# A filter loop whose transfers are cut into smaller ones and tied to places in the chunk

## The chip, the cores and the metric

The kernel runs on one core of a Trainium2 chip. The metric is the time on the device in microseconds, from one launch to its end. Engines are named as in the profile: PE (TensorE, with PEld for its weight loads), DVE (VectorE), ACT (ScalarE), POOL (GpSimd), SP (SyncE, which here only issues transfers).

## What is computed

The program takes `x` of 8 x 32 x 32 x 128 floats through two layers. Layer 0 is attention over 1024 tokens of each of 8 images. Layer 1 adds a state-space model run in both directions, and then a spectral filter. Only this last part is touched by the change:

```python
def _compute_spectral(u, sigma, phi, Mpp, Mpm):
    U_plus, U_minus = _stu_conv(phi, u, PADDED_SL)
    s = sigma ** SIGMA_POW
    out = jnp.einsum('btkd,k,kde->bte', U_plus, s, Mpp)
    out = out + jnp.einsum('btkd,k,kde->bte', U_minus, s, Mpm)
    return out
...
t = _to_tokens(x)
...
t = t + _L1_ffn_ref(_ln_t(t), L1_ffn_sigma, L1_ffn_phi, L1_ffn_M_u, L1_ffn_M_phi_plus, L1_ffn_M_phi_minus, L1_ffn_log_weights, L1_ffn_gumbel)
x = _from_tokens(t, x)
```

Here `_stu_conv` convolves each channel of the tokens with 16 filters, through Fourier transforms. The sum over filters and input channels may be done at each frequency: for every frequency a 128 x 128 matrix over the channels is applied to the spectra of the tokens, and the result is transformed back.

## The kernel before

The kernel is one straight program of about 47,600 instructions. Its last part, from line 1588 on, is in two stages.

**The filter loop.** The 128 frequencies (`NF`) go in 16 chunks of 8 (`FC`). For a chunk `c` there are two jobs. *Matrices*: `matrices` (line 1600) multiplies the filters' taps with the filter matrices, which lie in `mst`, into PSUM tiles `pg`; four copies per call, alternately by ACT (line 1613) and DVE (line 1611), bring them to SBUF as `gs`. *Apply*: `apply` (line 1634) multiplies the matrices with the spectra `u` into `py`, and `gather` (lines 1649 to 1655) forms sums and differences: one copy by ACT (`half`), then additions by DVE. A pair of gathers makes one tile `sums` of 128 rows, which is written to `yd` in device memory.

The loop runs one chunk ahead with the matrices: in round `c` it makes the matrices of chunk `c + 1` and applies those of chunk `c`. Each round has four steps `n`: two calls of `matrices`, then two of `apply` and one `gather`. Steps 0 and 1 make the first half of the chunk's frequencies, steps 2 and 3 the second. The order on PE, DVE, ACT and POOL is that in which the program is written (`manual_schedule` with these four in `IN_ORDER`); the order on SP is left to a scheduler.

**The loop's transfers, all issued by SP.** Each chunk needs its spectra: two loads of 256 KB (line 1620), each in rows of 256 bytes, after which POOL makes a negated and a plain copy (lines 1623 and 1624, once per chunk over the whole tile). Each chunk stores two tiles of sums of 256 KB (line 1657). When both stores of a chunk have landed, two early reads of 64 KB (line 1665, `fetch`) bring the part of `yd` that the last stage needs first into `early_yt`: 8 partitions per chunk. In the last round, which makes no matrices, the residuals are loaded from `xa`: 2 MB into `res1`, which takes the place of `mst`, and 1 MB into `room`, which takes the place of a `gs` (line 1668).

**The last stage.** After the loop come six reads of 1 MB of `yd` into `room` (line 1709) with one load of 1 MB of residuals among them, the inverse transform on PE (line 1725), the addition of the residuals by DVE (line 1732) and five stores of the output, issued by ACT (line 1735).

A tile's tag has so many buffers: `gs` and `u` two, `sums` three. A transfer that fills a buffer waits for its last readers.

Of the kernel before, what the change touches and what calls it, by code (L numbers as in the profile page):

```python
# [10 lines left out]
ALU = mybir.AluOpType  # L11
# [4 lines left out]
B = 8  # L16
# [14 lines left out]
NB = 2  # L31
NF = 128
FC = 8
PI_1024 = 0.0030679615757712823
IN_ORDER = {
    mybir.EngineType.PE,
    mybir.EngineType.DVE,
    mybir.EngineType.Activation,
    mybir.EngineType.Pool,
}  # L40
ALL_IN_ORDER = IN_ORDER | {mybir.EngineType.SP}
# [4 lines left out]
def fast_kernel(ctx: ExitStack, tc: tile.TileContext, a: dict, out: bass.AP, bad: bass.AP):  # L46
    nc = tc.nc
# [15 lines left out]
    def ctile(shape, name):  # L63
        pool = passing
        if name in LASTING:
            pool = const
        elif name in ("fwd", "m_u"):
            pool = resid
        elif name in ("wqkv", "bout", "group", "row_le", "row_ge"):
            pool = starting  # L70
        return pool.tile(shape, F32, tag=name, name=name)
# [8 lines left out]
    ud = dram.tile([NF // FC, P, B, NB, 2, 4, FC], F32, name="ud")  # L80
    yd = dram.tile([NF, NB, B, 2, 4, C], F32, name="yd")
# [23 lines left out]
    for d, m in enumerate((row_le, row_ge)):  # L105
        t = ctile([P, L], f"upto{d}")
        for c in range(2):
            rows = slice(c * L, (c + 1) * L)
# [504 lines left out]
    with ExitStack() as s:  # L613
# [172 lines left out]
        sums = {}  # L786
# [85 lines left out]
        for n in range(len(units) + 2):  # L872
            if n < len(units):
                prs[n] = scores(*units[n])
            if 2 <= n and units[n - 2][2] % 2:
                b, half, j = units[n - 2]
# [3 lines left out]
            if 1 <= n < len(units) + 1:  # L880
                b, half, j = units[n - 1]
# [42 lines left out]
    with ExitStack() as s:  # L924
# [12 lines left out]
        for d in range(2):  # L937
            nc.gpsimd.memset(up[d], 0.0)
            for c in range(2):
                rows = slice(c * L, (c + 1) * L)  # L940
# [57 lines left out]
        def behind(instruction, other, reason):  # L998
            tc.add_manual_dep(
                instruction.ins,  # L1000
                other.ins.name,
                mybir.DependencyInfo(mybir.DependencyClass.Sync, mybir.DependencyReason.DATA),
                reason=reason,
            )
# [360 lines left out]
        for at, u in enumerate(units[:-1]):  # L1365
# [41 lines left out]
            b = (u.b + 2) % B  # L1407
# [34 lines left out]
        u = units[-1]  # L1442
# [71 lines left out]
    with ExitStack() as s:  # L1514
        mp = s.enter_context(tc.tile_pool(name="c_m", bufs=1, side="right"))
        mst = mp.tile([P, 32, C], F32, tag="mst", name="mst")
        early_yt = mp.tile([P, 2, 4, 4, C], F32, name="early_yt")
# [67 lines left out]
        with ExitStack() as s2:  # L1585
# [4 lines left out]
            turn = 0  # L1590

            def matrices(c, n, gs):

                nonlocal turn
                pts = [ps_g.tile([P, 4, P], F32, tag="g", name=f"pg{c}_{n}_{g}") for g in range(4)]
                cols = slice(c * FC, (c + 1) * FC)
                for e in range(4):
                    for g in range(4):
                        rows = slice(g * 32, (g + 1) * 32)
                        nc.tensor.matmul(  # L1600
                            pts[g][:, e, :],
                            lhsT=mst[rows, n * 4 + e, :],
                            rhs=taps[rows, cols].rearrange("p f q m i -> p (f q m i)"),
                            start=True,
                            stop=True,
                        )
                for g, pt in enumerate(pts):
                    to = gs[:, :, n * 16 + g * 4 : n * 16 + g * 4 + 4]
                    frm = pt.rearrange("p e n -> p n e")
                    if turn % 2:  # L1610
                        nc.vector.tensor_copy(to, frm)  # L1611
                    else:
                        nc.scalar.copy(to, frm)  # L1613
                    turn += 1

            def loaded_spectra(c):

                u = p2.tile([P, 2, NB, B, 2, 4 * FC], F32, tag="u", name=f"u{c}")
                for k in range(NB):
                    nc.sync.dma_start(  # L1620
                        u[:, 0, k].rearrange("p b i f -> p b (i f)"), ud[c][:, :, k].rearrange("p b i q f -> p b (i q f)")
                    )
                nc.gpsimd.tensor_scalar(u[:, 1, :, :, 0, :], u[:, 0, :, :, 1, :], -1.0, None, ALU.mult)  # L1623
                nc.gpsimd.tensor_copy(u[:, 1, :, :, 1, :], u[:, 0, :, :, 0, :])
                return u

            def apply(c, n, q, gs, u, py):

                mats = gs.rearrange("p (f q m i) e -> p f q m i e", f=FC, q=4, m=NB)
                for m in range(NB):  # L1630
                    for i in range(2):
                        for t in range(4):
                            f = n * 4 + t
                            nc.tensor.matmul(  # L1634
                                py[t * 32 : t * 32 + 32 - 16 * m, q // 2, :],
                                lhsT=u[:, i, m:, :, :, q * FC + f].rearrange("p k b i -> p (k b i)"),
                                rhs=mats[:, f, q, m, i, :],
                                start=(m == 0 and i == 0),
                                stop=(m == NB - 1 and i == 1),
                            )  # L1640

            def gather(c, n, turn, py):

                if turn == 0:
                    gathered["sums"] = p3.tile([P, 4, C], F32, tag="sums", name=f"sums{c}_{n}")
                    gathered["both"] = p2.tile([P, 2, C], F32, tag="both", name=f"both{c}_{n}")
                sums, both = gathered["sums"], gathered["both"]
                half = p2.tile([P, C], F32, tag="half", name=f"half{c}_{n}_{turn}")
                nc.scalar.copy(half, py[:, 1, :])
                nc.vector.tensor_tensor(both[:, turn, :], py[:, 0, :], half, ALU.add)  # L1650
                nc.vector.tensor_tensor(sums[:, 2 + turn, :], py[:, 0, :], half, ALU.subtract)
                if turn == 0:
                    return
                nc.vector.tensor_tensor(sums[:, 0, :], both[:, 0, :], both[:, 1, :], ALU.add)
                nc.vector.tensor_tensor(sums[:, 1, :], both[:, 0, :], both[:, 1, :], ALU.subtract)
                at = c * FC + n * 4
                nc.sync.dma_start(
                    yd[at : at + 4].rearrange("f k b i q e -> (f k b i) (q e)"), sums.rearrange("p q e -> p (q e)")
                )

            def fetch(c):

                rows = slice(c * FC, (c + 1) * FC)
                for i in range(2):
                    nc.sync.dma_start(early_yt[rows, i], yd[rows, 0, 0:4, i])

            def load_residuals(k, b, n):
                nc.sync.dma_start(  # L1668
                    res[k][:, b : b + n].rearrange("p b r c -> p b (r c)"),
                    xa[b : b + n, :, k].rearrange("b p r c -> p b (r c)"),  # L1670
                )

            chunks = NF // FC
            gs, us, gathered = {}, {}, {}
            s2.enter_context(tc.manual_schedule(engines=IN_ORDER))
            for c in range(-1, chunks):
                if c + 1 < chunks:
                    gs[c + 1] = p2.tile([P, P, C], F32, tag="gs", name=f"gs{c + 1}")
                    us[c + 1] = loaded_spectra(c + 1)
                else:  # L1680

                    room = p2.tile([P, P, C], F32, tag="gs", name="room")
                    res = [room[:, :32, :], mp.tile([P, 32, C], F32, tag="mst", name="res1")]
                    res = [t.rearrange("p (b r) c -> p b r c", b=B) for t in res]
                    load_residuals(1, 0, B)
                    load_residuals(0, 0, 4)

                for n in range(4):
                    if c + 1 < chunks:
                        matrices(c + 1, 2 * n, gs[c + 1])  # L1690
                        matrices(c + 1, 2 * n + 1, gs[c + 1])
                    if c >= 0:
                        half, turn = divmod(n, 2)
                        py = ps_g.tile([P, 2, C], F32, tag="g", name=f"py{c}_{n}")
                        apply(c, half, turn, gs[c], us[c], py)
                        apply(c, half, turn + 2, gs[c], us[c], py)
                        gather(c, half, turn, py)
                if c > 0:
                    fetch(c - 1)
            fetch(chunks - 1)  # L1700


            pieces = [(k, h) for k in range(NB) for h in range(2)]
# [8 lines left out]
            for yt, (k, h) in zip(yts, pieces):  # L1712
# [6 lines left out]
                for b in range(0, 4, size):  # L1719
                    bs = slice(b, b + size)  # L1720
                    to = res[blk][:, h * 4 + b : h * 4 + b + size]
# [825 lines left out]
```

## Time and profile before

| | us |
|---|---|
| median of 3 runs | 1401.35 |
| the three runs | 1397.77, 1401.35, 1403.96 |
| the profiled execution, own time | 1397.79 |
| its span, first to last instruction | 1396.1 |
| before the filter loop | 0 to 1071.6 |
| filter loop, first matrices to the end of the last product | 1071.6 to about 1352 |
| last stage | about 1352 to 1396.1 |

The span is the time from the first to the last instruction of the profiled execution; 1.7 us lie around it. A line of groups names line, engine and operation, then what is written and read. In a line of the time line the columns are start, duration, engine, line, operation, how many instructions are merged, and in brackets the idle time before it with what ended it; "issue" there means that the profile shows nothing that the engine waited for. DMA queue q1 carries the transfers that SP issues, q8 instructions. These are the sizes of the loop's transfers:

```profile
u<-ud SPq DMA_DIRECT2D x32, 256.0 KB
yd<-sums SPq DMA_DIRECT2D x32, 256.0 KB
...
early_yt<-yd SPq DMA_DIRECT2D x32, 64.0 KB
res<-xa SPq DMA_DIRECT2D x1, 2048.0 KB
room<-xa SPq DMA_DIRECT2D x2, 1024.0 KB
```

### The profile page before, as it was taken

How to read it: one execution, taken by the hardware profiler on the slowest of the kernel's cores; microseconds unless marked ns; L12 is line 12 of the kernel's file. 1: busy time of each engine (PE TensorE's matmuls, PEld its weight loads, DVE VectorE, ACT ScalarE, POOL GpSimd, SP SyncE). 2: the span in 40 equal slices, each digit the busy share in tenths (PEclk: the TensorE clock that was granted, in tenths of full speed). 3: DMA queues.
4: the chain of work that ended last, by engine and by line, in shares of the span. 5: the costliest groups of instructions: out<-in, count | busy, mean ns of one | idle time of the engine just before them, and what ended most of it. 6: DMA issues, size and time to landing. Idle time of an engine off the chain costs nothing. (4 is left out here: it accounts for less than half of the span.)

```text
span 1396.1 us, 47569 instructions
## 1 busy us (share of the span) xinstructions
PE 1322.0 (95%) x20926; PEld 840.1 (60%) x20926; DVE 1094.0 (78%) x2140; ACT 926.1 (66%) x1432; POOL 534.1 (38%) x510
## 2 busy tenths in 40 slices
PE   7999999999999899999999999998798999999977
PEld 3333333333333666666666666666698988888964
DVE  6789888788778698989889888997554777777745
ACT  5767667766766788888878888875553655555520
POOL 3312976886910443434343343443673111111100
PEclk9999999999999999999999999999999999999989
DMA  7200111111101434444444443431578122222358
GB/s 173 56 2 2 39 39 39 54 39 39 31 1 40 99 79 95 112 96 109 94 108 92 93 94 91 115 83 47 166 220 219 45 71 72 72 71 72 79 179 303
DMA packets 139391, 123.24 MB, mean 88 GB/s; under 512 B 44808, under 2 KB 118152, under 8 KB 135080
## 3 DMA queue, kind: packets, MB, share of 16 engines
q1 hardware_dynamic: 137048, 115.93, 32.4%
q8 instruction: 166, 2.72, 0.8%
q10 hardware_dynamic: 2128, 4.19, 0.8%
q14 instruction: 49, 0.40, 0.1%
HBM read 78.15 MB, written 34.08 MB: 80 GB/s over the span
## 5 line engine op out<-in xcount | busy, mean ns | idle before, releaser
L803 ACT ACTIVATE pr<-pt 128x1024 f32<-128x1024 f32 x256 | 248.0, 1021 | 103.1 <-PE pt L798 102.1
L1613 ACT COPY gs<-pg 128x512 f32<-128x512 f32 x256 | 133.2, 601 | 69.9 <-PE pg L1600 54.8
L1611 DVE COPY gs<-pg 128x512 f32<-128x512 f32 x256 | 159.1, 684 | 20.6 <-PE pg L1600 16.7
L828 DVE TENSOR_TENSOR two<-pr,pr 128x1024 f32<-128x1024 f32 x128 | 164.3, 1324 | 13.4 <-ACT pr L803 13.4
L798 PE MATMUL pt<-q,k 32*128 32x512 f32 x1024 | 160.3, 640 | 6.1 <-ACT pr L803 4.2
L1600 PE MATMUL pg<-taps,mst 32*128 32x128 f32 x4096 | 149.2, 281 | 7.8 <-issue 4.6
L1600 PEld LDWEIGHTS pg<-taps,mst 32*128 32x128 f32 x4096 | 134.7, 188 | 22.4 <-issue 17.3
L819 PE MATMUL po<-pr,v 128*32 128x512 f32 x1024 | 139.9, 604 | 0.0
L1634 PE MATMUL py<-gs,u 128*32 128x128 f32 (+1 forms) x4096 | 129.9, 280 | 2.3 <-issue 2.2
L1024 POOL TENSOR_TENSOR ec<-ec,ct 128x2048 f32<-128x2048 f32 x16 | 83.6, 5228 | 112.4 <-ACT ct L1104 49.8
L1066 DVE SCALAR_TENSOR_TENSOR xs<-xp,cw,xs 128x1024 f32<-128x1024 f32 x96 | 122.4, 1282 | 2.2 <-issue 0.2
L1634 PEld LDWEIGHTS py<-gs,u 128*32 128x32 f32 (+1 forms) x4096 | 113.6, 141 | 10.1 <-issue 2.8
L1088 PE MATMUL pb<-bxt,wbc 128*128 128x512 f32 x256 | 114.0, 597 | 3.6 <-ACT zs L1079 3.6
L1623 POOL TENSOR_SCALAR u<-u 128x512 f32<-128x512 f32 x16 | 24.0, 1500 | 233.0 <-DMA u<-ud 121.1
L798 PEld LDWEIGHTS pt<-q,k 32*128 32x128 f32 x1024 | 49.0, 183 | 88.8 <-ACT pr L803 27.5
L1187 DVE SCALAR_TENSOR_TENSOR state<-state,dec,pst 128x64 f32<-128x64 f32 x448 | 87.3, 275 | 1.1
L1296 POOL TENSOR_TENSOR rms<-rms_v,mhalf 128x8 f32<-128x8 f32 x16 | 27.2, 1698 | 156.6 <-DVE rms_v L1294 156.6
L1088 PEld LDWEIGHTS pb<-bxt,wbc 128*128 128x128 f32 x256 | 47.1, 189 | 60.4 <-issue 55.0
L819 PEld LDWEIGHTS po<-pr,v 128*32 128x32 f32 x1024 | 27.7, 109 | 88.1 <-issue 84.8
L1010 POOL TENSOR_TENSOR lm<-cs,lm 128x2048 f32<-128x2048 f32 x16 | 57.9, 3621 | 58.1 <-DVE xs L1066 34.7
L839 PE MATMUL pd<-two,ones 128*32 128x512 f32 x512 | 74.0, 614 | 2.4 <-DVE two L828 2.2
L1266 PEld LDWEIGHTS spo<-wo,y 128*128 128x128 f32 x512 | 62.1, 191 | 15.3 <-issue 10.2
(305 smaller groups left out, 2768.9 us busy)
## 6 DMA issues: line engine op xcount, KB each, us to landing
lm<-cd SPq DMA_DIRECT2D x32, 512.0 KB
ec<-cd SPq DMA_DIRECT2D x32, 512.0 KB
ud<-sp SPq DMA_DIRECT2D x8, 1024.0 KB
u<-ud SPq DMA_DIRECT2D x32, 256.0 KB
yd<-sums SPq DMA_DIRECT2D x32, 256.0 KB
moved<-state SPq DMA_DIRECT2D x48, 128.0 KB
room<-yd SPq DMA_DIRECT2D x6, 1024.0 KB
X<-in_x SPq DMA_DIRECT2D x8, 512.0 KB
```

What stands on the lines that cost most here:

```text
L798: nc.tensor.matmul(pt[:, i, :], lhsT=k[rows, j * P : (j + 1) * P], rhs=q[rows, cols], start=True, stop=True)
L803: nc.scalar.activation(pr[:, 2 * g : 2 * g + 2, :].rearrange("p i t -> p (i t)"), pt.rearrange("p i t -> p (i t)"), AF.Exp, scale=SCALE,)
L819: nc.tensor.matmul(po[rows, :], lhsT=vs[b][:, j, rows], rhs=pr[:, h, :], start=(j == 0), stop=(j == NT - 1))
L828: nc.vector.tensor_tensor(two, sums["pr"][:, 2 * g : 2 * g + 2, :], pr[:, 2 * g : 2 * g + 2, :], ALU.add)
L1024: t = nc.gpsimd.tensor_tensor(u.ec, u.ec, u.ct.unsqueeze(1).to_broadcast([P, NH, NT, L]), ALU.mult)
L1066: u.convolved = nc.vector.scalar_tensor_tensor(acc, xp[:, at : at + T], cw[u.d][:, n, i : i + 1], acc, ALU.mult, ALU.add)
L1088: nc.tensor.matmul(u.pb[:, i * 512 : (i + 1) * 512], lhsT=wbc[u.d][:, k, :], rhs=xt[:, at : at + 512], start=(k == 0), stop=(k == KC - 1),)
L1187: nc.vector.scalar_tensor_tensor(u.state[:, k, h, :], u.state[:, k - 1, h, :], u.dec[:, c, h, j : j + 1], u.pst[c][:, j, h, :], ALU.mult, ...
L1600: nc.tensor.matmul(pts[g][:, e, :], lhsT=mst[rows, n * 4 + e, :], rhs=taps[rows, cols].rearrange("p f q m i -> p (f q m i)"), start=True, ...
L1611: nc.vector.tensor_copy(to, frm)
L1613: nc.scalar.copy(to, frm)
L1634: nc.tensor.matmul(py[t * 32 : t * 32 + 32 - 16 * m, q // 2, :], lhsT=u[:, i, m:, :, :, q * FC + f].rearrange("p k b i -> p (k b i)"), rhs ...
```

## The change

Each transfer of the loop is made smaller or single, and is given a place. A round has eight slots, two for each step `n`: slot `2n` follows the matrices' copies, slot `2n + 1` the gather. `passing_by` issues what belongs to the slot. `behind` adds a wait of the transfer for the copy named: in an even slot the last copy of the matrices, in an odd one ACT's copy of `half`.

- The spectra of the next chunk come in four loads of 128 KB (one of two blocks, one half of the batch), in slots 1, 2, 4 and 5. After each, POOL makes the negated and the plain copy of that quarter. Before, a chunk's spectra could be loaded as soon as the buffer was free.
- The sums are stored in two halves of 64 rows (128 KB): the first half at once in slots 3 and 7 (without an added wait), the second half in slot 6, and in slot 0 of the next round.
- The early reads of the chunk before go one by one, in slots 2 and 4.
- The residuals go in six loads of 512 KB, one in each of the last round's first six slots. That round makes no matrices, so its even slots have no copy to wait for.
- SP's instructions now keep the order in which the program is written (`ALL_IN_ORDER`).

```diff
+            def behind(instruction, other):
+                tc.add_manual_dep(
+                    instruction.ins,
+                    other.ins.name,
+                    mybir.DependencyInfo(mybir.DependencyClass.Sync, mybir.DependencyReason.DATA),
+                    reason="spaced transfers",
+                )
...
-                for k in range(NB):
-                    nc.sync.dma_start(
-                        u[:, 0, k].rearrange("p b i f -> p b (i f)"), ud[c][:, :, k].rearrange("p b i q f -> p b (i q f)")
-                    )
-                nc.gpsimd.tensor_scalar(u[:, 1, :, :, 0, :], u[:, 0, :, :, 1, :], -1.0, None, ALU.mult)
-                nc.gpsimd.tensor_copy(u[:, 1, :, :, 1, :], u[:, 0, :, :, 0, :])
...
+            def load_part(u, c, part, other=None):
+            
+                k, h = divmod(part, 2)
+                bs = slice(4 * h, 4 * h + 4)
+                t = nc.sync.dma_start(
+                    u[:, 0, k, bs].rearrange("p b i f -> p b (i f)"), ud[c][:, bs, k].rearrange("p b i q f -> p b (i q f)")
+                )
+                if other:
+                    behind(t, other)
+                nc.gpsimd.tensor_scalar(u[:, 1, k, bs, 0, :], u[:, 0, k, bs, 1, :], -1.0, None, ALU.mult)
+                nc.gpsimd.tensor_copy(u[:, 1, k, bs, 1, :], u[:, 0, k, bs, 0, :])
...
-                at = c * FC + n * 4
-                nc.sync.dma_start(
-                    yd[at : at + 4].rearrange("f k b i q e -> (f k b i) (q e)"), sums.rearrange("p q e -> p (q e)")
-                )
...
+            def store(c, n, h, sums, other=None):
+
+                at = c * FC + n * 4 + 2 * h
+                t = nc.sync.dma_start(
+                    yd[at : at + 2].rearrange("f k b i q e -> (f k b i) (q e)"),
+                    sums[64 * h : 64 * h + 64].rearrange("p q e -> p (q e)"),
+                )
+                if other:
+                    behind(t, other)
...
-            s2.enter_context(tc.manual_schedule(engines=IN_ORDER))
+            s2.enter_context(tc.manual_schedule(engines=ALL_IN_ORDER))
+            late_sums, waiting = {}, []
+
+            def passing_by(c, n, place, made):
+
+                slot = 2 * n + place
+                if slot in (3, 7):
+                    half = n // 2
+                    store(c, half, 0, gathered["sums"])
+                    late_sums[c, half] = (gathered["sums"],)
+                if slot == 6:
+                    store(c, 0, 1, *late_sums.pop((c, 0)), made)
+                if slot == 0 and c > 0:
+                    store(c - 1, 1, 1, *late_sums.pop((c - 1, 1)), made)
+                if c + 1 < chunks and slot in (1, 2, 4, 5):
+                    load_part(us[c + 1], c + 1, (1, 2, 4, 5).index(slot), made)
+                if c > 0 and slot in (2, 4):
+                    fetch(c - 1, (2, 4).index(slot), made)
+                if c + 1 == chunks:
+                    for _ in range(min(1, len(waiting))):
+                        waiting.pop(0)(made)
...
-                    load_residuals(1, 0, B)
-                    load_residuals(0, 0, 4)
+                    for k, b in [(1, 0), (1, 2), (1, 4), (1, 6), (0, 0), (0, 2)]:
+                        waiting.append(lambda made, k=k, b=b: load_residuals(k, b, 2, made))
 
                 for n in range(4):
+                    made = None
                     if c + 1 < chunks:
                         matrices(c + 1, 2 * n, gs[c + 1])
-                        matrices(c + 1, 2 * n + 1, gs[c + 1])
+                        made = matrices(c + 1, 2 * n + 1, gs[c + 1])
                     if c >= 0:
+                        passing_by(c, n, 0, made)
                         half, turn = divmod(n, 2)
                         py = ps_g.tile([P, 2, C], F32, tag="g", name=f"py{c}_{n}")
                         apply(c, half, turn, gs[c], us[c], py)
                         apply(c, half, turn + 2, gs[c], us[c], py)
-                        gather(c, half, turn, py)
-                if c > 0:
-                    fetch(c - 1)
-            fetch(chunks - 1)
+                        made = gather(c, half, turn, py)
+                        passing_by(c, n, 1, made)
+            store(chunks - 1, 1, 1, *late_sums.pop((chunks - 1, 1)))
+            for i in range(2):
+                fetch(chunks - 1, i)
```

## The prediction

> **What bounds the kernel now.** I read the page first (shares and the chain), then the core's spans by stretch, then the waits inside the filter loop, then the time line of single chunks, and last the DMA view of half-microsecond slices of them.
>
> ```profile
> span 1396.1 us, 47569 instructions
> ...
> PE 1322.0 (95%) x20926; PEld 840.1 (60%) x20926; DVE 1094.0 (78%) x2140; ACT 926.1 (66%) x1432; POOL 534.1 (38%) x510
> ...
> PE pg L1600 10%; PE py L1634 9%; PE pf L565 1%; DMA room<-yd 1%; PE pu L595 1%; ACT ln_x L483 1%; PE cpt L554 1%; DVE sd L576 0%; PE pz L1725 0%; SPq L1709 0%; ACT me L1534 0%; DMA xa<-X 0%; DVE b_st L467 0%; SPq L1668 0%; POOL sp L583 0%
> ```
>
> TensorE is the bound, and the two matmul lines of the filter loop (1600, 1634) lead the chain. The change touches only this loop, 1071.6 to 1353 us, and what follows. Cut into chunks (columns: PE, PEld, DVE, ACT, POOL busy, clock, DMA share, GB/s) it shows:
>
> ```profile
> 1094.60:1111.10 16.50, 16.50 (x518) 15.27 (x517) 12.43 (x29) 9.35 (x21) 2.06 (x2) 1.00 0.29 76
> ...
> 1145.30:1162.90 17.60, 17.01 (x522) 15.37 (x518) 12.58 (x29) 9.65 (x21) 2.05 (x2) 1.00 0.27 71
> ...
> 1213.90:1231.60 17.70, 16.87 (x521) 15.31 (x520) 12.56 (x29) 9.36 (x21) 2.07 (x2) 1.00 0.27 70
> ...
> 1300.40:1316.80 16.40, 16.40 (x520) 15.15 (x519) 12.51 (x29) 9.28 (x21) 2.06 (x2) 1.00 0.29 76
> ...
> sum 238.60, PE 233.90 PEld 213.69 DVE 175.61 ACT 131.33 POOL 28.88; mean PE 16.71 PEld 15.26 DVE 12.54 ACT 9.38 POOL 2.06
> ```
>
> A chunk that nothing disturbs takes 16.4 us and fills PE; nine of fourteen take 16.9 to 17.7. 14 x 16.4 = 229.6, so 238.6 - 229.6 = 9.0 us are lost, 4.7 of them as visible PE idle time (238.6 - 233.9). The waits name no engine for it, and one chunk shows it:
>
> ```profile
> PEld pg L1600 <- issue: 17.3, 66, 1.0
> ```
>
> ```profile
> 1138.72 1.16 PE L1600 MATMUL pg<-taps,mst 32*128 32x128 f32 x29
> 1140.67 1.38 PE L1600 MATMUL pg<-taps,mst 32*128 32x128 f32 x35 [0.79 <-issue]
> ```
>
> ```profile
> 1134.77 0.52 SPq L1620 DMA_DIRECT2D u<-ud  x1
> 1136.00 0.34 SPq L1657 DMA_DIRECT2D yd<-sums  x1
> 1136.39 0.52 SPq L1620 DMA_DIRECT2D u<-ud  x1
> 1140.81 0.63 SPq L1665 DMA_DIRECT2D early_yt<-yd  x2
> ```
>
> The gap is in mid-group, its place moves from 35 to 55 matmuls before the group's end over the loop, and it comes about 2 to 5 us after two u loads and a store (768 KB) were issued within 1.6 us. In the DMA view of 1138.0 to 1138.5 the instruction queue appears:
>
> ```profile
> q1 hardware_dynamic: 368, 0.11, 95.0%
> q8 instruction: 1, 0.02, 11.9%
> ```
>
> One such packet comes at 1128.4, 1132.6, then at 1138.2 where about 1136.7 was due: 1.5 us late, behind the burst. PE goes on 2.47 us after the late packet's start. The same holds at 1224.1 (PE again at 1226.69) and 1215.4 (1217.80). So a group of 128 matmuls ends a block of instructions every 4.11 us, a block is usable about 2.5 us after its packet starts, and there are 1139.88 - (1136.7 + 2.5) = about 0.7 us of slack. A burst that holds the packet back longer shows as a stall.
>
> The loop's end, from the chain:
>
> ```profile
> 1343.64 2.24 issue
> 1345.88 5.33 PE py L1634 x106
> ...
> 1352.86 2.24 DMA yd<-sums
> ...
> 1358.19 3.13 SPq L1668
> ...
> 1361.37 2.59 SPq L1709
> ...
> 1364.00 19.07 DMA room<-yd
> ```
>
> Residual loads of 2 MB (issued at 1338.23) and 1 MB (1341.90) saturate the DMA engines until about 1349.5; PE stalls for a block (2.24 us) and restarts on a low clock (0.81, then 0.62). The last sums land at 1352.86 + 2.24 = 1355.1; from there 6 MB of sums and 1 MB of residuals set the end.
>
> **What the Trainium skill says.** "Runtime: NRT & Kernel Launch", Instruction fetch mechanics: instructions come in blocks of 256 (16 KiB) by the sequencer's own DMA queue, the crossing "mostly hidden". The trace agrees on the block (0.02 MB packets) and shows where it isn't hidden. "DMA: Bandwidth & Descriptors", Queues, rings and completion order: each DMA engine serves its rings in turn, packet by packet. The trace has the fetch wait 1.5 us all the same, so I reckon with what is queued ahead. "TensorE: Matmul & The Clock Gate", Part 1: after idling TensorE gets half its clock for some 3.4 us of work; the clock of 0.62 after the 2.24 us stall fits.
>
> **The change part by part.** The instruction order of PE, DVE and ACT is unchanged; SP becomes a written order, POOL gets four pairs of operations per chunk where it had one.
>
> *Loads of spectra.* 2 x 256 KB become 4 x 128 KB, behind slots 1, 2, 4, 5 of the chunk (a slot: after the matrices' last copy, or after the copy of half the sums). Same bytes and 256-byte rows, so no data time is added. SP issues 4 x about 0.3 instead of 2 x 0.52 us and has over 10 us free in a chunk. The first load took from 1136.0 to 1137.2 for 256 KB, so a half is about 0.6 us of the engines. For the block fetch this means: instead of 1.5 us of delay, at most about 0.6, which is just under the slack of 0.7.
>
> *Sums by halves, early reads singly.* 128 KB and 64 KB each, at slots 3, 6, 7, next 0, and 2, 4. A 256 KB store alone delayed one packet (1215.4) into a 0.26 us stall; its half should not. The early reads wait for stores that were issued about 4.6 us before, where a landing takes 2.24 us: no stop for SP.
>
> *What is queued behind these waits.* SP is in order, so a late copy holds up everything behind it, the next chunk's spectra above all. The last quarter is issued 0.4 us after the third matmul group, its data takes about 1.0 to start and 0.6 to move, 0.9 passes until POOL starts (as 1294 to 1296.47 shows), and POOL needs between a quarter of and all of 1500 + 618 ns, 0.5 to 2.1 us; I take 0.95. It is ready 3.9 us after that group and needed 4.11 + 2.17 = 6.3 us after it. Cover 2.4 us; if it is gone, 1 us per us and chunk, 15 times. POOL's idle time (14 of 16.4 us) hides its four pairs at either bound.
>
> *What remains of the stalls.* Two of the four blocks in a chunk meet a half load. Bounds: none left (gain 9.0), or all as now (gain 0). I take 0.07 us for each of 28, 2.0 us, so 7.0 us are gained.
>
> *The start.* The second chunk's spectra are no longer loaded up front (1075) but during chunk 0, when DMA is nearly free: nothing either way.
>
> *The end.* The residual loads come later: SP places the first behind the last store of chunk 14, about 1342.3 instead of 1338.2, in 512 KB pieces. From 1342.5 the engines have to move 0.26 MB of sums, 3.15 of residuals, 0.13 of early reads, 0.26 of sums: 3.8 MB at the 385 to 390 GB/s of these stretches, 9.7 us, and 0.5 for a bubble while SP waits for a landing before the early read; with the last 0.26 MB they end at 1353.4 and land at 1354.4. PE no longer stalls at 1343.64 (its block is asked for at about 1339.7, before any load), so its sums are done by about 1349.1 instead of 1352.8; they then stand behind loads. Hence 0.7 us gained, not 3.7. Bounds -1.5 (the early reads, which fill only 8 partitions, hold the queue) to +1.5. What follows (reads in the same order, 1355.1 to the end) only shifts.
>
> *Sum.* Own time of the profiled execution 1397.79 - 7.0 - 0.7 = 1390.1. It is 3.56 us under the median of 1401.35; if the difference is more of these stalls, it goes too (1390.1), if not, it stays (1393.7). I take the middle, 1391.9.
>
> **The rivals.** A: the stalls stay or move to other blocks, since a fetch now always has some transfer beside it; only the end gains: 1401.35 - 0.7 = 1400.6. For it: half loads start where the fetch packets stand (1.3 to 2.2 us into a group), and the slack is no larger than a half load. Against it: chunks whose packets came ahead of the burst ran at exactly 16.4 us with the same bytes.
>
> B, slower: the half load together with the early read of the slot before it delays the fetch by 1.0 us instead of 0.6, at two blocks of every chunk, also in the five that are now free of stalls. Idle time costs 9.0/4.7 = 1.9 times itself, so 28 x (1.0 - 0.7) x 1.9 = 16 us are lost where 9.0 are now: 1401.35 + 7.0 - 0.7 = 1407.7. It decides from a delay of 0.7 + 9.7/(28 x 1.9) = 0.88 us. For it: the early read goes to 8 partitions and its data straggles for 1.5 us (1141.5 to 1143). Against it: 192 KB in all, spread over two slots.
>
> C: the last quarter lands over 2.4 us late and PE waits at each chunk's first product; with 0.5 us each about 7.5 us lost, net 1408.1 if the stalls' gain stays out. I see nothing that would delay it so.
>
> **How the numbers follow.** Forecast 0.60, A 0.26, B 0.10, C 0.04. About 0.5% (7 us) is what a measurement of this kernel tells from none. Of the forecast's 0.60, which runs from 1385 (all stalls gone, end +1.5, and the median's surplus gone) to 1396, some 0.05 lies above 1394.3: faster 0.55. A and that part, with a little of B: same 0.34. Slower 0.11. Cutting B and C and the lowest end gives 1385 to 1403.
>
> **What would show it.** Right: chunks all near 16.4 to 16.6 us, "issue" before matmul loads down to some 8 us in total, instruction packets 4.1 us apart, last sums issued near 1342 (own time line minus 7 for the loop) and the loop's end without an issue gap over 1 us. Wrong: chunks of 17 us with gaps at other places (A, B), PE waiting for u (C), or SP's stores of the last sums landing later than before.

## The result, and the profile after

| | before | after |
|---|---|---|
| median of 14 runs each, taken side by side | 1404.37 us | 1405.62 us |
| lowest and highest | 1397.77 to 1410.67 | 1396.76 to 1410.26 |
| profiled execution, own time | 1397.79 | 1408.89 |

The ratio after to before is 1.0008, with a 95% interval of 0.9989 to 1.0028: no change that can be measured. The prediction was 1391.9, and the measured median lies above its range (1385 to 1403). Among the rivals, A (the stalls move to other blocks) is nearest, but it also counted on a gain at the end, and there was a loss.

The page of the changed kernel (busy time by engine, then the chain of waits by line):

```profile
span 1407.2 us, 47841 instructions
...
PE 1329.7 (94%) x20926; PEld 843.6 (60%) x20926; DVE 1094.7 (78%) x2140; ACT 925.5 (66%) x1432; POOL 549.1 (39%) x606
...
PE pg L1600 10%; PE py L1649 8%; PE pz L1777 2%; PE pf L565 1%; PE pu L595 1%; ACT ln_x L483 1%; DMA yd<-sums 1%; PE cpt L554 0%; DVE sd L576 0%; DMA res<-xa 0%; DMA xa<-X 0%; ACT me L1534 0%; DMA early_yt<-yd 0%; DVE b_st L467 0%; POOL sp L583 0%
```

PE has gained 7.7 us of busy time and its share has fallen; `DMA yd<-sums`, `DMA res<-xa` and `DMA early_yt<-yd` are new in this line of the chain. The two spans differ by 11.1 us, far more than the two medians, so before any reading the difference was cut into stretches: to the loop's first matrices, on to the first product, fourteen chunks, on to the end of the last matrices, to the landing of the last sums, to the end.

| stretch (us) | before | after | after minus before |
|---|---|---|---|
| span's start to the first matrices | 1071.56 | 1076.78 | +5.2 |
| to the first product | 15.63 | 17.78 | +2.2 |
| fourteen chunks ("the loop" below) | 238.62 | 239.32 | +0.7 |
| to the end of the last matrices | 12.39 | 12.61 | +0.2 |
| to the landing of the last sums ("the end" below) | 16.90 | 19.44 | +2.5 |
| to the span's end | 40.96 | 41.23 | +0.3 |

The first row is code that the change doesn't touch. Over the fourteen traces taken in all, it runs from 1071.6 to 1079.4 us whatever the loop is. The second row is a longer wait of PE for ACT (3.74 instead of 2.23 us). It was not there in a second trace of the changed kernel (15.57), and it was there in one whose loop is that of before (17.54), so it isn't the change's either. What can be the change's is in "loop" and "end", and from here on only these two are compared.

The loop, in stretches of one chunk (PE, PEld, DVE, ACT, POOL busy, clock, DMA share, GB/s), for the changed kernel:

```profile
1094.56:1110.88 16.32, 16.32 (x514) 15.05 (x513) 12.19 (x29) 9.18 (x20) 3.08 (x8) 1.00 0.23 51
1110.88:1127.58 16.70, 16.70 (x513) 15.37 (x512) 12.53 (x29) 9.39 (x21) 3.07 (x8) 1.00 0.33 75
1178.19:1195.54 17.35, 16.78 (x513) 15.34 (x512) 12.54 (x29) 9.33 (x21) 3.07 (x8) 1.00 0.32 73
1299.73:1317.45 17.72, 16.58 (x516) 15.17 (x513) 12.46 (x29) 9.49 (x21) 3.08 (x8) 1.00 0.28 64
1317.45:1333.88 16.43, 16.43 (x513) 15.18 (x512) 12.51 (x29) 9.29 (x21) 3.03 (x8) 1.00 0.35 76
```

An undisturbed chunk still takes 16.4 us, and twelve of the fourteen are longer than that (16.65 to 17.8). Before, three quarters of the lost time (6.4 of 8.5 us) lay in the step after a chunk's first product (intervals between products of 4.3 to 5.2 us where 4.11 is undisturbed), and most of the rest in the third step. Now it is in all four (3.3, 1.6, 1.7 and 2.8 us): the four intervals of the chunk at 1299.73 are 4.63, 4.11, 4.86 and 4.12. The waits of the whole span say the same, here the changed kernel's, where there were 17.3 us before:

```profile
PEld pg L1600 <- issue: 16.0, 66, 1.0
```

One stall of the changed kernel, in its time line and then in the DMA queues of 1178.0 to 1178.5 (packets, MB, share of 16 engines) and of the half microsecond after it:

```profile
1180.14 0.94 PE L1600 MATMUL pg<-taps,mst 32*128 32x128 f32 x21
1181.64 1.60 PE L1600 MATMUL pg<-taps,mst 32*128 32x128 f32 x43 [0.57 <-issue]
```

```profile
q8 instruction: 1, 0.02, 21.1%
```

```profile
q1 hardware_dynamic: 45, 0.09, 87.8%
```

The first share is that of a single packet of instructions: 21.1% of 16 engines for 0.5 us is 1.69 us. It came 4.35 us after the one before it, so hardly late, but it lasted 1.69 us, where packets with no other transfer beside them last 0.88 to 1.47 (all the traces below). Right after its start a half store of sums fills q1. It ends at 1178.45 + 1.69 = 1180.14, and PE goes on 1.50 us later. In the stall at 1138 that the prediction shows, the packet came 1.5 us late and lasted 0.95; PE went on 1.49 us after its end. So a long packet holds PE as surely as one that comes late. The trace of before had one too, which the prediction passed over: this stall, at which the packet came 4.39 us after the one before it and lasted 1.68 us (21.0% of 1232.0 to 1232.5) beside a store of 256 KB.

```profile
1235.48 0.73 PE L1600 MATMUL pg<-taps,mst 32*128 32x128 f32 x17 [0.47 <-issue]
```

```profile
q8 instruction: 1, 0.02, 21.0%
```

The end of the loop, from the chain of the changed kernel:

```profile
1347.42 1.11 issue
...
1350.25 2.37 DMA yd<-sums
...
1353.10 6.68 DMA res<-xa
...
1359.80 6.13 DMA yd<-sums
...
1366.07 3.40 DMA early_yt<-yd
```

PE's big stall here (2.24 us before) has indeed shrunk, to 0.26 and 0.90 us, and the last product ends 10.7 us after the last matrices instead of 13.4. (In the second trace of the changed kernel a stall of 2.22 us is back, and it is 12.1 us.) But the last store goes out late and lands late. The last sums are written by 1358.44:

```profile
1358.16 0.28 DVE L1670 TENSOR_TENSOR sums<-both 128x128 f32<-128x128 f32 x1
```

The store's first half is issued at once, the second at 1359.80: by the chain, SP held it until the residual load issued at 1353.10 had landed. It then takes 6.13 us to land where the last store before took 2.24. Against before that is 2.7 us sooner for the last sums, 1.3 later for the issue and 3.9 later for the landing: 2.5 us lost.

### The profile page after: what moved, and what is told of

Read it like the earlier page. It is cut to its first block, busy times and chain, and to the rows that moved or that the text cites. A ratio compares the mean times of both kernels' runs of the same rounds, so it can differ in the third digit from the quotient of the medians.

```text
span 1407.2 us, 47841 instructions
## 1 busy us (share of the span) xinstructions
PE 1329.7 (94%) x20926; PEld 843.6 (60%) x20926; DVE 1094.7 (78%) x2140; ACT 925.5 (66%) x1432; POOL 549.1 (39%) x606
## 5 line engine op out<-in xcount | busy, mean ns | idle before, releaser
L1639 POOL TENSOR_SCALAR u<-u 128x128 f32<-128x128 f32 x64 | 34.1, 532 | 229.5 <-DMA u<-ud 200.1
```

## The experiments

Twelve further runs were made, two of them of the kernels unaltered; the rows "before" and "after" are the two traces already read. "Loop" and "end" are the stretches defined above; an undisturbed loop is 14 x 16.43 = 230.0 us.

| kernel | loads of spectra | stores | loop | end | time of its run |
|---|---|---|---|---|---|
| before | two | whole | 238.6 | 16.9 | 1397.79 |
| before_again | two | whole | 240.1 | 17.3 | 1405.92 |
| late_residuals | two | whole | 238.1 | 18.2 | 1408.31 |
| halves_alone | two | halves | 236.8 | 17.6 | 1402.66 |
| whole_sums | four | whole | 242.2 | 18.8 | 1408.50 |
| spaced_alone | four | whole | 245.4 | 17.6 | 1413.36 |
| after | four | halves | 239.3 | 19.4 | 1408.89 |
| after_again | four | halves | 239.4 | 19.3 | 1403.82 |
| tail_early | four | halves | 237.8 | 18.4 | 1407.22 |
| residuals_first | four | halves | 235.3 | 18.5 | 1405.55 |
| no_loads | none | halves | 232.3 | 19.4 | 1402.40 |
| by_phase | four, other places | halves | 234.4 | 20.3 | 1403.12 |
| phase_and_end | four, other places | halves | 236.6 | 18.3 | median 1400.96 |
| best_of_all | four, other places | whole | 232.5 | 19.9 | median 1405.85 |

**The scatter first: before_again and after_again**, the two kernels unaltered.

> The kernel before once more, for a second trace. Theory (its loop loses as much as the changed kernel's, in another place): loop stretch 236 to 240 us (first trace 238.6), stalls mostly in the step after the spectra's burst, end stretch 16 to 18 (first trace 17.0). Rival (the first trace of before was a bad one and its loop is normally free of stalls, so that the change costs the loop time): loop 230 to 234.

> The changed kernel once more, for a second trace. Loop stretch = from the first product of chunk 0 to that of chunk 14 (before 238.6 us, changed 239.3; 14 undisturbed chunks are 230.0). End stretch = from the end of the last matrices to the landing of the last sums (before 17.0, changed 19.4). Theory (the stalls for instruction blocks stay and only move to other blocks; the late residual loads hold up the last sums): loop 237 to 241, stalls spread over all four steps of a chunk, end 18.5 to 20.5. Rival (the first trace of the changed kernel was an unlucky one, the change does take the stalls away): loop 231 to 235.

Loop 240.1 and 239.4, end 17.3 and 19.3. The end repeats within 0.4 us. In the four kernels with the changed loop, it is this loop that scatters, from 235.3 to 239.4 (mean 238.0); in the three with the loop of before it is 238.1 to 240.1 (mean 238.9). So the mean loop is 0.9 us shorter, well inside the scatter, and the end costs 19.35 - 17.1 = 2.3: net +1.4, which fits the +1.1 us (0.0008) of the ratio and lies inside its interval. One loop of one kernel can differ by 4 us from trace to trace, so a single trace shows no smaller difference. The traces come from at least three chips, and what a chip adds to the scatter isn't known.

**Do the transfers hold the blocks? no_loads** leaves out the loads of spectra inside the loop and POOL's copies of them: all chunks use the first one's spectra.

```diff
-                    us[c + 1] = loaded_spectra(c + 1)
+                    us[c + 1] = loaded_spectra(c + 1) if c < 0 else us[0]
```

> The changed kernel without the loads of spectra inside the loop and POOL's copies of them: every chunk uses the spectra of chunk 0. Theory (the stalls are instruction blocks held up by the loop's transfers): half of the loop's bytes go, loop stretch 231 to 235 us instead of 239.3. Rival 1 (the stalls do not come from transfers): loop 237 to 241. Rival 2 (only the stores of sums hold blocks up): loop 236 to 240, stalls only at packets beside stores.

The loop as one stretch:

```profile
1095.02:1327.34 232.32, 231.92 (x7170) 213.14 (x7169) 175.35 (x393) 130.50 (x280) 0.00 (x0) 1.00 0.19 42
```

Only 2.3 us over the undisturbed loop are left, and PE idles for 0.4 us in all. This lies 3 us under the shortest of the four changed loops. So most of the stalls come with the loads of spectra, where the change puts them; the block's size or the order of instructions alone doesn't make them. It is a single trace, though, and best_of_all below, with all its loads at other places, is as short. Stores by halves and single early reads, which are still there, do little by themselves. POOL's copies are gone as well, and that they play no part wasn't tried by itself; but every stall counted below ends a fixed while after a packet of instructions.

**Which part does what: halves_alone and spaced_alone**, each the kernel before with one part of the change, and **whole_sums**, the changed kernel with its sums stored whole, at once.

```diff
 # halves_alone, against before
+                for h in range(2):
+                    nc.sync.dma_start(
+                        yd[at + 2 * h : at + 2 * h + 2].rearrange("f k b i q e -> (f k b i) (q e)"),
+                        sums[64 * h : 64 * h + 64].rearrange("p q e -> p (q e)"),
+                    )
 # spaced_alone, against before
+                        if c >= 0 and n in (1, 2):
+                            load_part(us[c + 1], c + 1, n, made)
...
+                        made = gather(c, half, turn, py)
+                        if c + 1 < chunks and n in (0, 2):
+                            load_part(us[c + 1], c + 1, 3 * n // 2, made)
 # whole_sums, against after
-                    half = n // 2
-                    store(c, half, 0, gathered["sums"])
-                    late_sums[c, half] = (gathered["sums"],)
+                    store(c, n // 2, gathered["sums"])
```

> The kernel before with every store of sums cut into two of 64 partitions, issued one after the other; all else as before. Theory (a half store costs the DMA engines 9.3 us of their time where a whole one costs 11.6, so the sums take 60% more of them): DMA share of the loop 0.32 instead of 0.27, loop unchanged within its scatter (238 to 241), end stretch 17.6 to 18.2 (0.6 more). Rival (halves are free at the end, only the late start of the residual loads counts): end 16.9 to 17.4.

> The kernel before with one part of the change alone: the spectra of the next chunk in four loads of 128 KB, each behind its copy, with their four pairs on POOL. Sums are stored whole, early reads and residual loads stay as before. Theory (a block's packet beside any transfer is stretched, so stalls move from step 1 to the other steps): loop 235 to 239.5 us, stalls (intervals of products over 4.4 us) in at least three of the four steps of the chunk, and the end stretch as before, 16.8 to 17.6. Rival (the four loads do clear the loop, and the halves with their cheap-looking stores eat the gain up): loop 231 to 234.5. Second rival (whole_sums says that four loads make the loop worse than two): loop 241 to 243.

> The changed kernel with the sums stored whole again (128 rows, 256 KB, at slots 3 and 7); all else as changed. Theory (a store of 64 rows holds the DMA engines nearly as long as one of 128, 9.3 against 11.6 engine-us in the two first traces, so that halving added load to the queue that the instruction blocks and the last sums share): DMA share of the loop stretch 0.27 to 0.28 instead of 0.32, end stretch 17.5 to 18.8 us instead of 19.4, loop stretch 233 to 237.5. Rival (a half takes half; the higher share comes from the other, smaller transfers): share 0.31 to 0.32, loop 237 to 240, end 19 to 20.

Loops: 236.8, 245.4 and 242.2. For whole_sums and spaced_alone the theory as written there is a miss: four loads beside whole stores are longer than either kernel, in spaced_alone beyond its second rival too. The loop of halves_alone is a little shorter than expected. With the rows of the table this makes a square: two loads and whole stores 238.9 (three traces), two loads and halves 236.8 (one), four loads and whole stores 242.2 and 245.4, four loads and halves 238.0 (four). The two with four loads and whole stores, one trace each, lie 3 to 6 us over the mean of before, and over every one of the seven traces with its loop or the changed one (240.1 at most). Beside halves four loads cost nothing clear. What halves do beside two loads is inside the scatter. So the part from which the whole gain was expected cost time in these traces, and the part to which none was given made up for it.

The packets of instructions, counted one by one over each loop (56 in each), agree with this. A packet of 1.5 us or more is called long here, since every one of these had another transfer beside it; one that starts over 4.6 us after the one before is called late.

| | loop | mean us | longest us | long | late |
|---|---|---|---|---|---|
| before | 238.6 | 1.11 | 1.68 | 1 | 14 |
| before_again | 240.1 | 1.23 | 1.82 | 11 | 11 |
| late_residuals | 238.1 | 1.25 | 2.13 | 7 | 11 |
| halves_alone | 236.8 | 1.17 | 1.57 | 1 | 13 |
| whole_sums | 242.2 | 1.29 | 1.89 | 13 | 8 |
| spaced_alone | 245.4 | 1.29 | 2.05 | 13 | 19 |
| after | 239.3 | 1.16 | 1.69 | 4 | 9 |
| after_again | 239.4 | 1.19 | 1.72 | 5 | 11 |
| tail_early | 237.8 | 1.24 | 1.74 | 4 | 9 |
| residuals_first | 235.3 | 1.14 | 1.46 | 0 | 7 |
| no_loads | 232.3 | 1.12 | 1.73 | 4 | 6 |
| by_phase | 234.4 | 1.14 | 1.65 | 1 | 8 |
| phase_and_end | 236.6 | 1.12 | 1.44 | 0 | 11 |
| best_of_all | 232.5 | 1.11 | 1.55 | 1 | 8 |

The loop goes with the two counts together: 7 to 14 in the loops under 237 us, 21 to 32 in those over 240. (A stall puts off the next packet, so some late ones are its effect.) In all 115 stalls of PE of over 0.15 us in these loops, PE goes on 1.22 to 1.72 us after a packet's end, also where the profile names ACT or DVE. The three traces with the loop of before have 1, 11 and 7 long packets and 11 to 14 late ones, the four of the changed loop 0 to 5 and 7 to 11. So the change makes late packets a little rarer, if anything, and removes neither kind; that it trades late ones for long ones, as the first two traces alone suggest, is not shown. Here is a stall of spaced_alone: the time line, and the queues of 1202.3 to 1202.6.

```profile
1203.81 0.93 PE L1600 MATMUL pg<-taps,mst 32*128 32x128 f32 x18
1205.85 1.61 PE L1600 MATMUL pg<-taps,mst 32*128 32x128 f32 x46 [1.11 <-issue]
```

```profile
DMA packets 203, 0.07 MB, mean 225 GB/s; under 512 B 202, under 2 KB 202, under 8 KB 202
...
q1 hardware_dynamic: 202, 0.05, 104.9%
q8 instruction: 1, 0.02, 38.2%
```

202 packets of 256 bytes, one quarter of the spectra, fill the engines (104.9%) beside the one packet of instructions, which starts at 1202.36 and lasts 1.84 us; PE goes on 1.65 us after its end. They are of the quarter of the spectra issued at 1200.83 (SP's order here is the scheduler's, and it often issues two quarters within 3 us): what the packet meets is the "half load" that the prediction held to be just small enough. Why fewer packets are long with halves than with whole stores beside four loads isn't shown by these runs; that no more than 128 KB stand in one burst is an explanation that was not tried by itself.

What a half store costs the DMA engines, however, can be read. Taken alone, a store of 256 KB took 17.8% of 16 engines over 4 us (before, 1095 to 1099), 11.4 us of engine time; one of 128 KB took 30.9% over 2 us (after, 1163 to 1165), 9.8 or 9.9. So two halves are 1.7 times a whole. The Trainium skill, "SBUF — State Buffer", states in Door 1: The DMA port swizzle that partitions 0 to 63 reach only 8 of the 16 ports, and in "Can I just issue two DMAs to hit both halves?" that two transfers can't be joined to use all; the figures agree in direction. The DMA share of the loop, at nearly equal bytes, shows it too: 0.26 in whole_sums, 0.27 before, 0.31 in halves_alone, 0.32 after.

**The end: late_residuals** is the kernel before with its residual loads in six pieces behind copies, as in the change.

```diff
-                    load_residuals(1, 0, B)
-                    load_residuals(0, 0, 4)
+                    pieces = [(1, 0), (1, 2), (1, 4), (1, 6), (0, 0), (0, 2)]
...
+                        if c + 1 == chunks and pieces:
+                            load_residuals(*pieces.pop(0), 2, made)
```

> The kernel before, with one thing of the change: the 3 MB of residual loads in six pieces behind the copies of the last two chunks' ends, as in the changed kernel, so that they start about 4 us later. Sums whole, early reads and loop as before. Theory (the DMA engines' work between the last matrices and the last sums sets this end; what starts later ends later): last product sooner after the last matrices (11 to 12 us instead of 13.4), the last sums' landing over 5 us after it instead of 3.5, end stretch 18 to 19. Rival (the end is lost by halves and by the early reads issued singly): end 16.8 to 17.5.

End 18.2, as the theory has it, and its two halves as well: the last product ends 11.7 us after the last matrices, and the landing, after which SP issues the early read of the last chunk, comes 6.5 us after that. SP's queue in this kernel:

```profile
1349.44 0.39 SPq L1679 DMA_DIRECT2D res<-xa  x1
...
1351.27 2.08 SPq L1679 DMA_DIRECT2D res<-xa  x3
...
1354.89 1.35 SPq L1679 DMA_DIRECT2D room<-xa  x2
1360.11 0.33 SPq L1666 DMA_DIRECT2D yd<-sums  x1
```

The last matrices end at 1347.1; the loads begin 2.3 us later, where before they began 0.1 us later. Later loads let PE finish sooner, but the last sums then stand behind them. One thing of the change, 1.1 us of the 2.3. halves_alone has an end of 17.6, 0.5 more than before, at the lower edge of what was expected; its chain shows two stalls of PE, as before_again has them (2.25 and 1.91 us), and the quick landing of the kernel before:

```profile
1347.93 2.31 issue
1350.24 3.76 PE py L1634 x115
1354.00 1.63 issue
...
1357.71 2.37 DMA yd<-sums
```

spaced_alone, too, is at 17.6. whole_sums, with no halves, ends at 18.8, 0.6 better than the changed kernel. The three parts alone sum to about 1.1 + 0.5 + 0.5 = 2.1 of 2.3, the last two hardly larger than what the end differs by between two traces of one kernel. What the early reads cost, issued singly in the midst of the residual loads, no run took alone; nor what SP's written order does, in which the last store waited for a residual load.

**Mending the end: residuals_first, tail_early.** residuals_first is the changed kernel with the residual loads in two, as early as before. tail_early spreads them from the last matrices on and puts the early reads of the last two chunks after the last store.

```diff
 # residuals_first, against after
...
+                        if (c, n) == (chunks - 2, 3):
+                            res1 = mp.tile([P, 32, C], F32, tag="mst", name="res1")
+                            res = [None, res1.rearrange("p (b r) c -> p b r c", b=B)]
+                            load_residuals(1, 0, B)
 # tail_early, against after
+                if (c, slot) == (chunks - 2, 7):
+                    load_residuals(1, 2, 2, made)
+                if c + 1 == chunks and slot in (1, 3, 5):
+                    for k, b in {1: [(1, 4), (1, 6)], 3: [(0, 0)], 5: [(0, 2)]}[slot]:
+                        load_residuals(k, b, 2, made)
...
+            for c in (chunks - 2, chunks - 1):
+                for i in range(2):
+                    fetch(c, i)
```

> The changed kernel with the residual loads as before: 2 MB at once behind the last matrices, 1 MB behind the last store of chunk 14; the early reads of chunk 14 keep their places. Theory A (the late start of the residual loads holds up the last sums): PE stalls again (2 us or more), yet the end stretch is 16.5 to 18 us instead of 19.4. Theory B (the early reads among the residual loads hold them up, wherever the loads start): 18.5 to 20.

> The changed kernel with only the end altered: the first residual load right behind the last matrices instead of behind the last store of chunk 14, the others spaced from there, and the early reads of chunk 14 behind the last store. Theory (at the end the late start of the residual loads and the early reads among them hold up the last sums): end stretch 13 to 15.5 us instead of 19.4, loop stretch unchanged at 237 to 241. Rival (the last sums land late whatever stands ahead, since their own halves are slow): end stretch 18 to 20.

They end at 18.5 and 18.4, 0.9 better than the changed kernel; tail_early is a miss. In residuals_first PE's stalls are back (1.73 and 2.77 us), as theory A had it, but the end is that of theory B. Whichever way the loads are placed, one of two things is late: PE, for its blocks, or the last store, behind the loads.

**Other places in the chunk: by_phase, phase_and_end, best_of_all.** by_phase issues the halves of loads and stores only behind the first and the last of a step's copies of the matrices. phase_and_end adds a paced end, and best_of_all has whole stores and the residual loads in two.

```diff
 # by_phase, against after
+                if place == 0:
+                    early, late = made or (None, None)
+                    if n == 0 and c > 0:
+                        store(c - 1, 1, 0, late_sums[c - 1, 1], early)
+                        store(c - 1, 1, 1, late_sums[c - 1, 1], late)
+                    if n in (1, 2) and c + 1 < chunks:
+                        load_part(us[c + 1], c + 1, 2 * n - 2, early)
+                        load_part(us[c + 1], c + 1, 2 * n - 1, late)
```

> The changed kernel with the same transfers, but each behind the first or the last copy of a step's matrices (1.9 and 3.3 to 3.8 us into a step) instead of behind the copy of half the sums (0.45 us into it). The packets of instruction blocks stand 1.2 to 3.0 us into a step, data starts about 1.0 us after an issue. Theory (what counts is whether a transfer's data stand beside the block's packet): loop stretch 231 to 235 us. Rival (the total of bytes in the loop counts, not their place): loop 237 to 241, as in the changed kernel.

> Transfers by phase as in the run of that name, and at the end the residual loads in pieces of 512 KB from the last matrices on, the last sums ahead of the early reads. Theory: loop stretch 233 to 236 us, PE stalls at the end under 1 us, end stretch 13.5 to 16.5; against before 3 to 8 us faster, ratio 0.994 to 0.998. Rival (the end is bound by the bytes between the last matrices and the last stage, so spacing gains nothing): end stretch 17 to 19.5, ratio 0.997 to 1.000.

> Whole sums, transfers by phase, and the end as before: residual loads of 2 MB behind the last matrices and 1 MB after, early reads of chunk 14 behind the last store. Theory: loop stretch 232 to 235.5 us (before 238.6 and 240.1), end stretch 16 to 17.5 (before 17.0 and 17.4), so 4 to 7 us faster than before, ratio 0.995 to 0.997. Rival (loop stretches scatter by 4 us between executions whatever the places, so the first by-phase trace was luck): loop 236 to 239, ratio 0.998 to 1.000.

Loops 234.4, 236.6, 232.5: their mean is 3.5 us below that of the changed loop, and two lie below its lowest. At most one packet of 56 is long in each. The ends of phase_and_end and best_of_all (18.3 and 19.9) are longer than their theories had them. Timed against the kernel before, phase_and_end is at 0.998 (0.9965 to 0.9995), a gain of 0.2%, and best_of_all at 1.0001 (0.9984 to 1.0018), none. That doesn't go with best_of_all's loop, the shortest of all with loads. The end, 2.8 us longer than before, takes back less than half of the 6.4 us; the rest must have been a chance of that one execution, whose own time of 1400.26 is 5.6 under the median, or be hidden in the scatter. The end is 19.9, with PE stalled for 2.16 us and then, in the last group of products of its time line,

```profile
1351.49 0.80 PE L1651 MATMUL py<-gs,u 128*16 128x128 f32 x9 [4.42 <-issue]
```

for 4.42 us. best_of_all has whole stores and four loads and yet no long loop, so the square above holds at most for the places that the change has, not for any. The runs leave open which places are good, and how much of these loops is chance.

## Why the prediction was wrong

- **What bounds the loop** was right: blocks of instructions held up by transfers (no_loads). That late packets alone make the stalls was only a part of it.
- **The step that failed** is in the loads of spectra: "instead of 1.5 us of delay, at most about 0.6, which is just under the slack of 0.7", and from it "I take 0.07 us for each of 28, 2.0 us, so 7.0 us are gained". It reckons the delay of the packet's start only, from "a block is usable about 2.5 us after its packet starts". In the stalls of that very trace PE goes on 2.32 to 3.23 us after the start, but 1.30 to 1.56 after the end: the length counts in full. In the changed loop packets lasted up to 1.69 to 1.74 us (after, after_again, tail_early) instead of 0.95, which by itself uses up the slack of 0.7. Nor did the delay stay under 0.6: packets still came up to 5.09 us (after) and 5.27 us (after_again) after the one before and stalled PE, where 4.11 is regular. Of 8.9 us of stalls 8.0 are left, not 2.0. In the kernel before, four loads alone made them 15.4 in one trace. A margin of 0.1 us between an estimated delay and an estimated slack was no ground for a chance of 0.60.
- **Sums by halves**: "its half should not" was a statement on one stall and had no price. With them the changed loop is 4 us shorter than whole_sums, each costs 9.8 instead of 5.7 us of engine time, and at the end the second half is issued about half a microsecond after the first.
- **What is queued behind the waits** was right. POOL took 0.53 + 0.29 us per quarter and its four pairs are hidden; PE waited for the last quarter only once, 0.26 us at the end (0.28 in the second trace). Rival C is out, and so is the start.
- **The end**: "Hence 0.7 us gained, not 3.7" came out as 2.3 us lost, beyond the bound of -1.5. PE's part was right in direction: the last product came 2.7 us sooner (about 1.4 in the second trace, with a stall of 2.22 us that should have gone). What failed is the store behind the loads. The transfers were put at 3.8 MB at 385 to 390 GB/s from 1342.5 on, with a landing 1.0 us after their end. In fact the first residual load came 4.5 us after the last matrices instead of 4.2, the last store waited 1.35 us to be issued and took 6.13 to land, and the engines moved 385 GB/s only in parts. In two stretches of the changed kernel in which early reads or stores lie among the residuals, the engines are full (share 1.10 and 1.06) at half that rate (last column); that these small transfers are the cause was not tried by itself:

```profile
1355.50:1356.50 1.00, 0.29 (x11) 0.04 (x4) 0.00 (x0) 0.00 (x0) 0.00 (x0) 1.00 1.10 166
...
1359.50:1361.00 1.50, 0.00 (x0) 0.00 (x0) 0.00 (x0) 0.00 (x0) 0.00 (x0) 1.00 1.06 198
```

- **The last stage only shifts**: right, 40.8 to 42.6 us from the landing to the end in every run.
- **Which rival**: A's mechanism (the stalls are left, in other blocks), with the end's sign turned. B (slower through early reads beside half loads) did not come: the loop is no slower, and the spread early reads are in no_loads too, whose loop is almost free of stalls.
- **The median's surplus** over the profiled execution was taken for stalls, half of them to go. Most of the scatter is before the loop: the first matrices come at 1071.6 to 1079.4. The median of three runs was itself 3.0 us under that of fourteen. So of the 13.7 us between the prediction and the measured median, 7.7 are the gain that didn't come, 1.2 the loss measured in its place, 1.8 the half of the surplus and 3.0 those three runs.

## What to carry to other kernels

A fetch of instructions can be late, and it can be long: measure a stall from the end of its packet, and price both, not only how large the largest burst is. Look at a second trace of the same kernel before a count is called an effect; here long packets went from 1 to 11 with nothing changed. When parts of a change act on the same resource, try each alone before pricing their sum; here the part meant to gain lost, and a part held to be neutral made up for it. Where two ends compete for the DMA engines, as here the blocks of PE and the last store, moving the bulk later only changes which of them is late.

## What the runs showed of the hardware that was not expected

- PE goes on 1.22 to 1.72 us after the packet of a block of instructions has ended, in all 115 stalls of the fourteen loops. The Trainium skill, "Runtime: NRT & Kernel Launch", Instruction fetch mechanics, calls the crossing "mostly hidden"; in the undisturbed chunks it is, but at the loop's end it cost up to 4.42 us at one block.
- A packet of 16 KB lasts 0.88 to 1.47 us when nothing is beside it (165 of the 784 packets of the fourteen loops), and up to 2.13 (late_residuals) beside other transfers.
- A store from 64 partitions costs 9.8 us of DMA engine time, one of twice the bytes from 128 partitions 11.4.
